# A due-time scheduler in a two-layer attention kernel: pacing of projection steps in cross attention

## The chip, the cores and the metric

The kernel runs on one core of one Trainium2 chip. The metric is the device time of one execution in microseconds (us); the times given are medians over the runs shown. The core's engines work in parallel, each in its own program order: PE (TensorE, matrix products; PEld are its weight loads), DVE (VectorE), ACT (ScalarE), POOL (GpSimd) and SP (SyncE, which here only issues DMA transfers). They wait for each other through semaphores.

## What is computed

Two layers of a transformer block, in float32, for 4 batches of 512 tokens of width 320, with 20 heads of width 16. Each layer is self attention, cross attention to a context of 1601 tokens of width 192, and a gated feed-forward stage:

```python
h1 = _ln(x, n1_g, n1_b)
x = _attn(h1, h1, q1, k1, v1, o1_w, o1_b, heads) + x
h2 = _ln(x, n2_g, n2_b)
x = _attn(h2, context, q2, k2, v2, o2_w, o2_b, heads) + x
h3 = _ln(x, n3_g, n3_b)
proj = h3 @ ff_w1 + ff_b1
a, g = jnp.split(proj, 2, axis=-1)
ff = a * jax.nn.gelu(g, approximate=False) @ ff_w2 + ff_b2
return ff + x
```

`_attn` projects queries, keys and values, takes `softmax(q k^T * dh**-0.5)` over the keys, multiplies with the values and projects with `wo`; `_ln` is a layer norm with scale and bias.

## The kernel before, in words

**Units.** The work is cut into 84 units, listed in order: for each layer 20 units of self attention and 20 of cross attention (4 batches by 5 groups of 4 heads; 64 columns of the projections to a group), then 4 feed-forward units. A cross unit has 13 chunks of up to 128 keys, a self unit 4. The Python program writes out every engine's instruction order by hand; there is no automatic scheduling behind it.

**A chunk** (`main`, the loop at its end) goes like this. First one round of products on PE: the scores of this unit's four heads, keys by queries (L1280; three passes a head, the last of which subtracts the row maxima kept in `nrows`), and woven between them the products of a later unit's heads, queries by keys (L1054, the last 65 keys L1081), whose row maxima are wanted before that unit may begin. PE works on four heads at a time, as each takes 32 rows. ACT raises the scores of the chunk (L1290, four instructions of 128x512). DVE reduces the products of the later unit to maxima (L1069, four instructions; L1091). Then come the values product of the chunk before (L1306), which ACT copies out (L1325; L1320 in chunk 0) and POOL adds to the unit's sum `o` (L1326, in chunks 1 to 12). Then `steps` runs some of the pending work.

**The maxima of the next unit.** `give` hands a chunk one pair of products for each half of its round, if the later unit's keys and queries have been moved four rounds ago (`at_hand`). A chunk without a pair leaves products over, and these are made up by an extra round (`round_of(extra[0])`) in another chunk. At the end of chunk 10, behind its steps, `max_reduce` and `max_end` finish the next unit's maxima on DVE: a reduction (L1109), a cast (L1119), a subtraction (L1120), both of 128x16 with their operands in SBUF, and a transpose (L1123); SP then copies them to `nrows` in four DMAs (L1131).

**Pending work** stands in eight queues (`chains`). Each entry has a cost (a rough PE time in us), a due round, a hard condition (`ready`) and a soft one (`soon`). There are two rounds to a chunk. `pick` takes, of the queues' first entries that may run, the one due first. The entries that cost 0.1 or more are the projection steps; in cross attention these are

- keys of a later unit, four pieces of 200 or 201 context columns (L951, copied out at L994 by DVE or L997 by ACT, whichever the program expects to be free sooner; after the fourth piece POOL splits them into a high and a low part, L803 and L804, 128x801, and four DMAs, L852, move them into place),
- its queries (L927, ACT L935, a split of 128x256 on POOL at L803 and L804, eight DMAs),
- values (L1015, copied out at L994 or L997), in two parts: the first for groups 0 and 1 (128 columns) and the second for groups 2 to 4 (192 columns), 13 steps each and batch,
- the output projection of an attention that has ended (L1209, added to `x` by DVE at L1216), eight steps a batch.

Entries of no cost or of 0.01 (`LIGHT`) are norms (statistics L546, normalisation L562 and L568), the context's transposes (L733), the affine part on POOL (L595), and the division. **The division**: when group 4 of a batch has ended, an errand loads the sums of the exponentials (L1158), DVE inverts them (`invert`), they are saved, another errand reads them back with the unnormalised output (L1183, L1184), and POOL multiplies (L1191, three instructions: the first two together, the third later). An errand is run by `carry`, at the end of `steps`, when the moves of keys and queries have left room in that round.

**Credit.** Each round adds to `clock["credit"]` what the due times ask for (`pace`, at least -2 and at most 4 in all), and each entry that runs takes its cost off. In `steps`, a step is run only if the credit is at least its cost times a factor: 0.5 for the first of a chunk, 0.75 for the second, 1.5 for the third, then 3.0 us. If the first of the queues cannot be afforded, `steps` ends for this chunk.

`add_proj` puts keys and queries into their queues three units ahead in cross attention (`u.early` marks the first cross unit of a layer, which is prepared during self attention); `add_values` puts in the two parts of the values.

Of the kernel before, what the change touches and what calls it, by code (L numbers as in the profile page):

```python
# [61 lines left out]
def slices(n, k):  # L62

    out, at = [], 0
    for i in range(k):
        w = n // k + (i < n % k)
        out.append((at, w))
        at += w
    return out


KCUT = slices(HALF, 4)
# [3 lines left out]
def kernel(ctx: ExitStack, tc: tile.TileContext, x, context, ws, out):  # L76
# [273 lines left out]
    units = []  # L350
# [29 lines left out]


    chains = {n: deque() for n in ("divide", "project", "norm", "scale", "context", "early", "proj", "values")}
    clock = {"round": 0, "credit": 0.0, "lights": 0, "tiles": None, "ff": False}
    ALIKE = ("project", "early", "proj", "values")
    LIGHT = 0.01
    stage = [0] * B
# [41 lines left out]
    def add(chain, cost, f, due, ready=yes, soon=yes):  # L428
        chains[chain].append((cost if isinstance(cost, tuple) else (cost,), due, ready, soon, f))
# [7 lines left out]
    def pick():  # L437
        heads = [
            (q[0][1] + late_by(n), n)
            for n, q in chains.items()  # L440
            if q and q[0][2]() and q[0][3]() and (q[0][0][0] != LIGHT or clock["lights"])
        ]
        return min(heads)[1] if heads else None

    def run(chain):
        costs, _, ready, _, f = chains[chain].popleft()
        assert ready(), chain
        f()
        clock["credit"] -= sum(costs)
# [19 lines left out]
    def tick():  # L469
        clock["round"] += 1  # L470
        clock["credit"] = max(-2.0, min(4.0, clock["credit"] + pace()))

    def steps(beside, lights=1):


        tick()
        clock["lights"] = lights
        clock["tiles"] = True if beside is None else None
        done = 0
        while True:  # L480
            name = pick()
            if name is None:
                break
            cost = sum(chains[name][0][0])
            if cost >= 0.1:
                share = (2.2, 1.1) if beside else (9.0, 9.0) if beside is False else (0.5, 0.75, 1.5)
                least = cost * share[done] if done < len(share) else 3.0
                if clock["credit"] < (3.0 if beside is False else least):
                    break
                done += 1  # L490
                if clock["tiles"] is not None:
                    clock["tiles"] = name in ALIKE
            run(name)
            if cost == LIGHT:
                clock["lights"] -= 1
        clock["tiles"] = None
        carry()
# [308 lines left out]
    def add_proj(u):  # L806
# [3 lines left out]
        keys_due = due - 10 if u.cross else due  # L810
# [55 lines left out]
        def keys_free():  # L866
            return not pending["k"]
# [110 lines left out]
        if not u.cross:  # L978
            for part in range(2):
                add(chain, (0.46,) * 3, lambda part=part: both(part), due - 2 + 2 * part, lambda part=part: part or staging_free())  # L980
        else:
            for part, (_, w) in enumerate(KCUT):
                add(
                    chain, 0.05 + w * 8 / 2400, lambda part=part: keys_of_context(part),
                    keys_due - 2 * (len(KCUT) - 1 - part), lambda part=part: part or keys_free(),
                )
            if u.g == 0:
                add(chain, 0.0, hold, due - 4, yes, lambda: "h" in u.own)
            add(chain, (0.477,) * 3, queries, due - 2, staging_free)
# [10 lines left out]
    def add_values(u):  # L1000

        parts_k = CK if u.cross else HK
        wv = wv2 if u.cross else wv1

        def values(i, c):

            h0, h1 = PARTS[i]
            w = (h1 - h0) * DH
            ps = bank("vps")
            r = min(P, u.nkeys - c * P)  # L1010
            written(0.1 + w * 4 * len(parts_k) / 2400, ps)
            at = c * P
            for k, _, n in parts_k:
                for f, m in tiles_of(r):
                    nc.tensor.matmul(  # L1015
                        ps[f : f + m, :w],
                        lhsT=u.kvT[:n, k, at + f : at + f + m],
                        rhs=wv[:n, k, h0 * DH : h1 * DH],
                        start=(k == 0),
                        stop=(k == len(parts_k) - 1),  # L1020
                    )
            taken(vals[:r, c, h0:h1, 0:DH], ps[:r, :w].rearrange("p (h d) -> p h d", d=DH), ps, 0.12 + w * 0.001)
            u.vmade[i] += 1

        for i, g in enumerate((0, 2)):

            user = attn[u.n - (4, 1)[i]] if u.n else None
            w = (PARTS[i][1] - PARTS[i][0]) * DH

            def free(c, user=user):  # L1030
                return u.kvT is not None and (user is None or user.valued > min(c, user.nch - 1))

            for c in range(u.nch):
                add(
                    "values", 0.05 + w / 600 * len(parts_k), lambda i=i, c=c: values(i, c),
                    units[u.i + g].start + 2 * c, lambda c=c, free=free: free(c),
                )


# [332 lines left out]
    def add_norms(i):  # L1372

        while norms and norms[0].i <= i + ((1 if norms[0].b else 3) if norms[0].kind == "ff" else AHEAD + 1 if norms[0].early else 8):
            u = norms.popleft()
            if u.kind == "ff":
                add_norm(u.l, u.b, 2, lambda t, u=u: setattr(u, "hT", t), lambda u=u: u in ff_read, u.start - (4 if u.b else 40))
            else:

                def done(u=u):  # L1380
                    return u.made["q"] == G and (u.cross or u.made["k"] == G and u.vmade[1] == u.nch)

                due = lead(u) - (10 if u.cross else 28)
                add_norm(u.l, u.b, int(u.cross), lambda t, u=u: u.own.update(h=t), done, due)
# [299 lines left out]
    for i, u in enumerate(units):  # L1684
        nxt = units[i + 1] if i + 1 < len(units) else None
        before(u)
        if u.kind == "ff":

            flush()
            now(loads)  # L1690
            loads.clear()
            until_normed(lambda: u.hT is not None)
        clock["ff"] = u.kind == "ff"
        add_norms(i)
        for k in (3, SOON, AHEAD):
            v = units[i + k] if i + k < len(units) else None
            if v is not None and v.kind != "ff" and k == (SOON if not v.cross else AHEAD if v.early else 3):
                add_proj(v)
                if v.g == 0:
                    add_values(v)  # L1700
        (ff_main if u.kind == "ff" else main)(u, giver(u), nxt)
# [27 lines left out]
```

## Time and profile before

| | before |
|---|---|
| time, median of 3 runs | 3000.69 us (3000.01 to 3001.19) |
| time of the profiled execution | 3000.91 us |
| its span, first to last instruction | 2999.1 us |
| mean granted clock of TensorE | 0.993 |
| cross attention of the first layer, about | 370 to 1232 us |
| cross attention of the second layer, about | 1850 to 2720 us |

The profile was taken of one execution. Its page gives busy time by engine, the clock that TensorE was granted, the chain of waits that ended last, and groups of equal instructions. In a row of the timeline stand start, duration, engine, line, operation, output and inputs with their shapes, and the count; in brackets the idle time of the engine before it and what ended it. In a row of busy time by stretch stand the stretch and its length, the busy time of PE, PEld, DVE, ACT and POOL with the instructions in brackets, the granted clock of TensorE as a share of full speed, the share of the DMA engines and their GB/s. In a row of a group stand the busy time, the mean duration in ns, and the idle time before.

### The profile page before, as it was taken

The page shows a single profiled execution, that of the slowest core. Times are in us where ns is not written, and L with a number is a line of the kernel's source. Part 1 is how long each engine was busy: PE and PEld are TensorE (multiplying, and loading weights), DVE is VectorE, ACT ScalarE, POOL GpSimd, SP SyncE. Part 2 cuts the span into 40 slices and gives each one's busy share as a digit, 9 for nine tenths or more (in the row PEclk, how much of TensorE's full clock was granted, in tenths as well). Part 3 has the DMA queues.
Part 4 walks back from the last instruction along what each step waited for, and adds up shares of the span by engine and source line. Part 5 has one row for each costly group of instructions (what it writes and reads, how often), then busy time and mean ns, then how long its engine had stood idle before and what let it go on. Part 6 is the DMA issues. An engine that isn't in the chain of part 4 may idle for free.

```text
span 2999.1 us, 84363 instructions
## 1 busy us (share of the span) xinstructions
PE 2885.4 (96%) x35018; PEld 1509.7 (50%) x35018; DVE 2150.8 (72%) x4143; ACT 1892.7 (63%) x3746; POOL 1194.0 (40%) x1305
## 2 busy tenths in 40 slices
PE   8999999999999999999999899999999999999999
PEld 4455554555554554355554555555555555544555
DVE  6877888889889888323268788888888888873221
ACT  3766677877877878501147676778778778784000
POOL 3444344544544545211224443445445454451110
PEclk9999999999999999999999999999999999999999
DMA  4444223132232122200123342222221121222000
GB/s 107 103 122 102 71 74 96 46 90 60 53 82 67 39 56 60 82 17 15 37 60 74 91 99 66 66 58 53 53 64 46 49 70 44 54 54 76 22 22 14
DMA packets 186543, 188.70 MB, mean 63 GB/s; under 512 B 69668, under 2 KB 137264, under 8 KB 186160
## 3 DMA queue, kind: packets, MB, share of 16 engines
q1 hardware_dynamic: 185368, 182.11, 24.0%
q8 instruction: 276, 4.52, 0.6%
q10 hardware_dynamic: 760, 1.18, 0.2%
q14 instruction: 107, 0.88, 0.1%
q0 software_dynamic: 32, 0.00, 0.0%
HBM read 55.76 MB, written 29.36 MB: 28 GB/s over the span
## 4 chain that ended last, share of the span: by engine, by line
PE 77%; DVE 18%; DMA 1%; issue 1%; ACT 1%; POOL 1%; SPq 1%; ACTq 0%; DVEq 0%; POOLq 0%
PE av L1306 21%; PE st L1280 15%; PE fps L1391 9%; DVE pm L1069 9%; PE sps L1054 6%; PE yps L1498 6%; PE vps L1015 4%; DVE nmax L1069 4%; PE ops L1209 3%; PE kps L951 3%; PE qkps L886 3%; PE fps L1451 2%; PE qps L927 2%; PE sps L1081 1%; DVE hturned L608 1%
## 5 line engine op out<-in xcount | busy, mean ns | idle before, releaser
L1290 ACT ACTIVATE pr<-st 128x512 f32<-128x512 f32 (+1 forms) x2720 | 1405.0, 603 | 429.1 <-PE st L1280 381.4
L1069 DVE TENSOR_REDUCE pm<-sps 128x1 f32<-128x512 f32 x1920 | 1185.3, 681 | 129.6 <-PE sps L1054 121.5
L1326 POOL TENSOR_TENSOR o<-o,vo 128x512 f32<-128x512 f32 x576 | 740.7, 1286 | 1125.9 <-ACT vo L1325 1114.3
L1054 PE MATMUL sps<-kT,q 32*128 32x512 f32 x4800 | 874.4, 429 | 13.7 <-DMA q<-low 4.3
L1306 PE MATMUL av<-pr,vals 128*32 128x512 f32 (+1 forms) x5440 | 738.4, 609 | 74.7 <-DVE nmax L1069 19.3
L1280 PE MATMUL st<-q,kT 32*128 32x512 f32 (+1 forms) x5120 | 795.7, 421 | 7.1 <-DVE pm L1069 6.4
L1280 PEld LDWEIGHTS st<-q,kT 32*128 32x128 f32 (+1 forms) x5120 | 422.9, 180 | 299.5 <-issue 120.1
L1280 PE MATMUL st<-nrows,ones 32*128 32x512 f32 (+1 forms) x2720 | 542.6, 399 | 5.4 <-DMA nrows<-turned 5.4
L1054 PEld LDWEIGHTS sps<-kT,q 32*128 32x128 f32 x4800 | 424.0, 183 | 102.2 <-DVE pm L1069 26.8
L1069 DVE TENSOR_REDUCE nmax<-sps 128x1 f32<-128x512 f32 x640 | 395.2, 680 | 81.1 <-PE sps L1054 77.9
L1325 ACT COPY vo<-av 128x512 f32<-128x512 f32 x576 | 352.3, 612 | 26.8 <-PE av L1306 24.7
L1462 ACT ACTIVATE gl<-fps,b 128x512 f32<-128x512 f32 x80 | 54.8, 687 | 414.3 <-PE fps L1451 303.0
L1306 PEld LDWEIGHTS av<-pr,vals 128*32 128x32 f32 (+1 forms) x5440 | 111.1, 108 | 348.8 <-DVE pm L1069 180.7
L1391 PE MATMUL fps<-hT,w 128*128 128x512 f32 x640 | 283.2, 597 | 0.0
L1280 PEld LDWEIGHTS st<-nrows,ones 32*128 32x128 f32 (+1 forms) x2720 | 247.0, 180 | 28.2 <-DMA nrows<-turned 4.8
L1463 DVE SCALAR_TENSOR_TENSOR hid<-fps,b,gl 128x512 f32<-128x512 f32 x80 | 59.7, 748 | 238.8 <-ACT gl L1462 236.7
L1391 PEld LDWEIGHTS fps<-hT,w 128*128 128x128 f32 x640 | 119.2, 190 | 155.1 <-issue 152.6
L1498 PE MATMUL yps<-w,hid 128*128 128x320 f32 x640 | 176.0, 435 | 0.1
L1498 PEld LDWEIGHTS yps<-w,hid 128*128 128x128 f32 x640 | 120.4, 190 | 56.4 <-ACT gl L1462 5.3
L1209 PEld LDWEIGHTS ops<-wo,aT 112*32 112x32 f32 (+1 forms) x3072 | 98.0, 110 | 64.6 <-issue 42.9
L1209 PE MATMUL ops<-wo,aT 112*32 112x160 f32 (+1 forms) x3072 | 126.2, 301 | 0.9 <-DVE pm L1069 0.9
L1505 DVE TENSOR_TENSOR x<-yps,x 128x320 f32<-128x320 f32 x32 | 15.7, 492 | 145.9 <-PE yps L1498 145.9
(89 smaller groups left out, 2476.1 us busy)
## 6 DMA issues: line engine op xcount, KB each, us to landing
kT<-stages SPq DMA_DIRECT2D x160, 200.2 KB
oway<-o SPq DMA_DIRECT2D x80, 256.0 KB
q<-high SPq DMA_DIRECT2D x160, 64.0 KB
q<-low SPq DMA_DIRECT2D x160, 64.0 KB
kT<-high SPq DMA_DIRECT2D x60, 128.0 KB
q<-high SPq DMA_DIRECT2D x60, 128.0 KB
kT<-low SPq DMA_DIRECT2D x57, 128.0 KB
aT<-oway SPq DMA_DIRECT2D x32, 224.0 KB
```

Of the source, the lines that this page charges most:

```text
L886: nc.tensor.matmul(ps[f : f + m, :w], lhsT=wqk[:n, k, f // GD, column : column + m], rhs=first.hT[:n, k, at : at + w], start=(k == 0), sto ...
L1015: nc.tensor.matmul(ps[f : f + m, :w], lhsT=u.kvT[:n, k, at + f : at + f + m], rhs=wv[:n, k, h0 * DH : h1 * DH], start=(k == 0), stop=(k == ...
L1054: nc.tensor.matmul(ps, lhsT=u.q[j * SLOT : (j + 1) * SLOT, e, t * P : (t + 1) * P], rhs=u.kT[j * SLOT : (j + 1) * SLOT, u.k0 + s * 512 : u ...
L1069: nc.vector.tensor_reduce(to[:, j : j + 1], ps, AX.X, ALU.max, negate=(ns == 1))
L1209: nc.tensor.matmul(ps[f : f + m, : D // 2], lhsT=aT[:n, k, f * NQ + t * SLOT : f * NQ + t * SLOT + m], rhs=wo[:n, k, cols], start=(k == 0) ...
L1280: nc.tensor.matmul(own[0][:r, :], lhsT=ones[rows, :r] if e == 2 else u.keys(rows, c), rhs=u.rows[rows, :] if e == 2 else u.q[rows, e, :], ...
L1290: nc.scalar.activation(p[:r], own[0][:r], AF.Exp)
L1306: nc.tensor.matmul(ps[j * SLOT : (j + 1) * SLOT, :], lhsT=columns_of[:r, head : head + SLOT], rhs=pr.pop((c, j))[:r, :], start=True, stop= ...
L1325: nc.scalar.copy(vo, ps)
L1326: nc.gpsimd.tensor_tensor(u.o, u.o, vo, ALU.add)
L1391: nc.tensor.matmul(ps, lhsT=w1[:, k, i * FF + c * P : i * FF + (c + 1) * P], rhs=natural(u.hT[:, k]), start=start, stop=stop,)
L1498: nc.tensor.matmul(ps[:, :D], lhsT=hid[c][:, t * P : (t + 1) * P], rhs=w2[:, c, :], start=(c == 0), stop=(c == NHC - 1),)
```

## The change

Three edits, none of which changes an instruction; they change which entries run in which chunk.

- **Share of credit in cross attention.** A flag `clock["cross"]` is set for each unit. In a cross unit's chunks the factors are -1.0, 1.0 and 1.5 instead of 0.5, 0.75 and 1.5: the first step runs unless the credit lies below minus its cost, the second needs its full cost.
- **Due rounds of the pieces of keys.** The four pieces of a cross unit's keys were due two rounds apart, counted back from the last; they are due five apart, but for the first cross unit of a layer. The last piece's due round stays.
- **Due rounds of the first part of the values.** In cross attention of batches 1 to 3 the steps of the first part are due 20 rounds sooner.

```diff
-    clock = {"round": 0, "credit": 0.0, "lights": 0, "tiles": None, "ff": False}
+    clock = {"round": 0, "credit": 0.0, "lights": 0, "tiles": None, "ff": False, "cross": False}
...
             if cost >= 0.1:
-                share = (2.2, 1.1) if beside else (9.0, 9.0) if beside is False else (0.5, 0.75, 1.5)
+                share = (2.2, 1.1) if beside else (9.0, 9.0) if beside is False else (-1.0, 1.0, 1.5) if clock["cross"] else (0.5, 0.75, 1.5)
                 least = cost * share[done] if done < len(share) else 3.0
                 if clock["credit"] < (3.0 if beside is False else least):
                     break
...
                 add(
                     chain, 0.05 + w * 8 / 2400, lambda part=part: keys_of_context(part),
-                    keys_due - 2 * (len(KCUT) - 1 - part), lambda part=part: part or keys_free(),
+                    keys_due - (2 if u.early else 5) * (len(KCUT) - 1 - part), lambda part=part: part or keys_free(),
                 )
...
                 add(
                     "values", 0.05 + w / 600 * len(parts_k), lambda i=i, c=c: values(i, c),
-                    units[u.i + g].start + 2 * c, lambda c=c, free=free: free(c),
+                    units[u.i + g].start + 2 * c - (20 if u.cross and g == 0 and u.b else 0), lambda c=c, free=free: free(c),
                 )
...
         clock["ff"] = u.kind == "ff"
+        clock["cross"] = u.cross
         add_norms(i)
```

## The prediction

> **What bounds the kernel now.** I read the page first, then busy time by stretch, then the timelines of single chunks. A unit is one group of four heads of one batch; I call a cross unit layer.batch.group, counted from 0, and its key chunks 0 to 12.
>
> ```profile
> span 2999.1 us, 84363 instructions
> PE 2885.4 (96%) x35018; PEld 1509.7 (50%) x35018; DVE 2150.8 (72%) x4143; ACT 1892.7 (63%) x3746; POOL 1194.0 (40%) x1305
> ...
> PE 77%; DVE 18%; DMA 1%; issue 1%; ACT 1%; POOL 1%; SPq 1%; ACTq 0%; DVEq 0%; POOLq 0%
> ```
>
> PE sets the end, and where it does not, DVE does. The change acts in cross attention, about 1700 of the 2999 us. Two 800 us stretches of it, then units 0.1.1, 0.1.2 and 0.1.3:
>
> ```profile
> core 0: us, PE busy (x) PEld busy (x) DVE busy (x) ACT busy (x) POOL busy (x), PEclk, DMA share, GB/s
> 400.00:1200.00 800.00, 770.80 (x10925) 406.03 (x10923) 693.40 (x1307) 627.05 (x1253) 390.43 (x382) 1.00 0.26 66
> 1900.00:2700.00 800.00, 772.45 (x10935) 405.39 (x10928) 677.43 (x1259) 632.73 (x1266) 392.71 (x382) 1.00 0.22 55
> ...
> 647.30:693.50 46.20, 44.73 (x696) 24.43 (x695) 40.38 (x84) 34.41 (x69) 20.81 (x19) 1.00 0.30 77
> 693.50:740.60 47.10, 44.04 (x660) 23.41 (x659) 43.31 (x85) 34.91 (x70) 20.91 (x29) 1.00 0.33 81
> 740.60:779.80 39.20, 38.64 (x536) 20.15 (x535) 31.55 (x60) 33.70 (x67) 24.62 (x24) 1.00 0.19 46
> ```
>
> PE stands idle for 29.2 and 27.6 us of the two stretches, 57 us in all: with PE's work unchanged, that and time at a lower clock are all there is to win. The first question is therefore whether moving steps out of crowded chunks into empty ones pays by itself. Two empty chunks (no step) of unit 0.3.3, and what a key step costs:
>
> ```profile
> 1181.18 2.07 ACT L1290 ACTIVATE pr<-st 128x512 f32<-128x512 f32 x4 [0.24 <-PE st L1280]
> 1183.10 0.62 ACT L1325 COPY vo<-av 128x512 f32<-128x512 f32 x1
> 1183.70 2.07 ACT L1290 ACTIVATE pr<-st 128x512 f32<-128x512 f32 x4
> ...
> 1186.43 1.08 ACT L1290 ACTIVATE pr<-st 128x512 f32<-128x512 f32 x2 [0.19 <-PE st L1280]
> ```
>
> ```profile
> 562.30 0.86 PE L951 MATMUL kps<-ctxT,w 96*32 96x200 f32 x16
> ```
>
> A chunk lasts from one group of exponentials to the next: 2.52 us, then 2.73. ACT's own work is 2.07 + 0.62 = 2.69, so an empty chunk is held by ACT and not by PE, but by only 2.63 (the mean) against 2.52. A step adds about its PE time in an empty chunk and in a crowded one alike. Spreading alone is worth about 0.1 us a chunk, so the answer must lie in single stalls.
>
> **The dearest repeated stall** is in chunks 10 and 11 of group 0 of batches 1 to 3 in both layers, six units. In unit 0.1.0 (POOL, DVE, PE, ACT in turn):
>
> ```profile
> 638.75 1.28 POOL L1326 TENSOR_TENSOR o<-o,vo 128x512 f32<-128x512 f32 x1 [1.73 <-ACT vo L1325]
> 639.99 2.52 POOL L1191 TENSOR_TENSOR aT<-aT,rT 112x512 f32<-112x512 f32 x2
> ...
> 639.09 0.98 DVE L1119 CAST parts<-nmax 128x16 fp32r<-128x16 f32 x1
> 640.11 1.21 DVE L1120 TENSOR_TENSOR parts<-nmax,parts 128x16 f32<-128x16 f32 x1
> ...
> 642.18 0.44 PE L1280 MATMUL st<-q,kT 32*65 32x512 f32 x2 [1.10 <-DVE pm L1069]
> ...
> 639.37 2.06 ACT L1290 ACTIVATE pr<-st 128x512 f32<-128x512 f32 x4 [0.69 <-PE st L1280]
> 643.58 2.05 ACT L1290 ACTIVATE pr<-st 65x512 f32<-65x512 f32 x4 [1.67 <-PE sps L1054]
> ...
> 647.31 1.08 ACT L1290 ACTIVATE pr<-st 128x512 f32<-128x512 f32 x2 [0.90 <-PE st L1280]
> ```
>
> max_end's cast ends at 640.07, as POOL's add ends at 640.03; its subtraction, 16 columns, then takes 1.21 us and ends at 641.32 with the first of the two divisions (639.99 + 1.26). DVE stands behind POOL, no bank is emptied, and PE waits 1.10. Chunk 11 lasts 643.58 - 639.37 = 4.21 us. An empty chunk 11 without a division, in unit 0.1.3:
>
> ```profile
> 768.57 2.07 ACT L1290 ACTIVATE pr<-st 128x512 f32<-128x512 f32 x4 [0.85 <-PE sps L1081]
> ...
> 771.17 2.07 ACT L1290 ACTIVATE pr<-st 128x512 f32<-128x512 f32 x4
> ...
> 773.75 2.07 ACT L1290 ACTIVATE pr<-st 128x512 f32<-128x512 f32 x4
> ```
>
> It lasts 2.58, so the hold costs 1.63. In unit 0.2.0 a second price follows:
>
> ```profile
> 855.90:859.30 3.40, 2.26 (x22) 0.77 (x15) 3.37 (x6) 1.73 (x4) 3.40 (x3) 1.00 0.22 58
> 859.30:862.70 3.40, 3.40 (x26) 1.08 (x25) 2.74 (x5) 2.25 (x5) 0.17 (x1) 0.63 0.31 89
> 862.70:866.10 3.40, 3.31 (x46) 1.41 (x40) 2.04 (x4) 1.84 (x5) 1.27 (x1) 0.87 0.09 31
> ...
> 859.31 2.05 ACT L1290 ACTIVATE pr<-st 65x512 f32<-65x512 f32 x4 [1.68 <-PE sps L1054]
> ...
> 864.64 1.57 ACT L1290 ACTIVATE pr<-st 128x512 f32<-128x512 f32 x3 [1.56 <-PE st L1280]
> ```
>
> After 3.4 us with 1.14 us of idle PE the clock falls to 0.63 and 0.87; chunk 12 lasts 5.33 against 647.31 - 643.58 = 3.73 in unit 0.1.0, 1.60 more.
>
> **The change part by part.** The order of both programs tells what moves. PE, POOL and SP issue the same instructions as before; a net five of the 432 copies of keys and values out of banks go from ACT to DVE, too few to price.
>
> The share of credit: of 520 cross chunks, 138 were empty and 60 took two steps; now 128 and 48. It is little, because the first step still waits while credit is below minus its cost. Ten fewer empties at 0.11 (0.2 where the next chunk pays too): **-1.5 us**.
>
> The key pieces, due five rounds apart: keys land earlier, so that chunks seldom lack their pair of maximum products, which an extra round makes up. Cross chunks with an extra round fall from 18 to 8; four of the ten only completed a chunk with half its pair and are costed at nothing (PE's products are the same, 0.2 either way). A whole one:
>
> ```profile
> 810.17 2.06 ACT L1290 ACTIVATE pr<-st 128x512 f32<-128x512 f32 x4 [0.23 <-PE sps L1081]
> ...
> 814.39 2.06 ACT L1290 ACTIVATE pr<-st 128x512 f32<-128x512 f32 x4 [0.48 <-PE st L1280]
> ...
> 817.73 2.05 ACT L1290 ACTIVATE pr<-st 65x512 f32<-65x512 f32 x4 [0.48 <-PE st L1280]
> ...
> 605.36 2.06 ACT L1290 ACTIVATE pr<-st 128x512 f32<-128x512 f32 x4 [0.66 <-PE st L1280]
> ...
> 608.33 2.07 ACT L1290 ACTIVATE pr<-st 128x512 f32<-128x512 f32 x4 [0.42 <-PE st L1280]
> ```
>
> The chunk with a value step and an extra round lasts 4.22, its partner with a key step and no pair 771.17 - 768.57 = 2.60, together 6.82; a plain key chunk (814.39 to 817.73) and a plain value chunk (605.36 to 608.33) 3.34 + 2.97 = 6.31. So 0.51, four times net, the other two of the six being replaced by whole rounds in group 1 of batch 0: **-2.0 us**.
>
> The earlier values, together with the other two, move the division. On SP the load of the sums (L1158) now stands behind the eight query moves that it preceded, so that invert, read and divide follow later. POOL's order in unit 0.2.0 around its adds (L1326; the x6 ends with add 9, and so does, after, the single one):
>
> ```
> before: L1326 x6 | L1191 x2 | L1326 x3 | L1191 | L803 L804 801 wide
> after:  L803 L804 801 wide | L1326 | L803 L804 256 wide | L1326 x3 | L1191 x2
> ```
>
> The pair goes from between add 9 and add 10, where max_end runs, to chunk 0 of the next unit, where DVE has reductions only, in all six units. Five holds go at 1.63 (8.15), with the 1.60 of clock; in unit 1.1.0 chunk 11 had a key step, and I count only what PE waited for the maxima:
>
> ```profile
> 2137.32 0.50 PE L1280 MATMUL st<-nrows,ones 32*128 32x512 f32 x2 [1.41 <-DMA nrows<-turned]
> ```
>
> In the new SP order those four copies go ahead of the division's loads. What POOL has near max_end instead are the splits:
>
> ```profile
> L803 POOL CAST stages<-stages 128x801 fp32r<-128x801 f32 x40 | 34.2, 856 | 43.3 <-ACT stages L997 16.6 <-DVE stages L994 10.9 <-DVE pm L1069 8.7
> L804 POOL TENSOR_TENSOR stages<-stages 128x801 f32<-128x801 f32 x40 | 64.1, 1603 | 3.2
> L803 POOL CAST high<-low 128x256 fp32r<-128x256 f32 x18 | 7.5, 419 | 0.3 <-ACT low L935 0.3
> ```
>
> In five units the key split stands before add 9, a chunk too early, and a query split behind it, in a chunk that the query step lengthens: 0 to 0.42 each; I take 0. In unit 0.1.0 it stands right behind add 9, so the subtraction waits for its 0.86. Together 8.15 + 1.60 + 1.41 - 0.86 = **-10.3 us**; if the splits hold fully (5 x 0.42), -8.2.
>
> The Trainium skill ("TensorE: Matmul & The Clock Gate", section The HAM clock gate) lets the clock drop after an idle window of about 3.4 us. Here 1.14 us of idle in such a stretch was followed by 0.63, so the trace differs; by the page the sum would lack the 1.60, and come to -8.7.
>
> Unpriced are the normalisation chunks of group 2: unit 0.1.2 is at 43.31 of 47.10 on DVE and now takes 18 steps instead of 15, unit 0.1.1 11 instead of 16. The six steps that move either fill PE's 3.1 idle us of unit 0.1.2 or stand behind DVE; I take 0, with 3 us either way over all such units, and one clock drop more or less.
>
> Sum: -1.5 - 2.0 - 10.3 = -13.8. The profiled execution took 3000.91 us (span 2999.1), 0.2 above the median of 3000.69; 3000.91 - 13.8 = 2987.1, as a median **2987 us**.
>
> **Rivals.**
> A, DVE decides in group 2. Eight such units (two layers, four batches) take normalisation with values and output projections in the same chunks. If each gains one stall of 1.1 us of idle PE and the 1.60 of clock, that is 8 x 2.7 = 21.6, and 2987 + 21.6 = 3009, slower. It decides from five such stalls on. For it: DVE's 92% there. Against: unit 0.1.1 is relieved, and the empty chunk behind the normalisation is now filled.
> B, POOL's holds only change their owner: the 801-wide split of 1.60 takes the place of the division's 1.26 at max_end. For it: it moves to chunks 8 to 10. Against: it is a chunk ahead. Then the 10.3 is nought: 2997. The Trainium skill ("SBUF — State Buffer", section Who interferes with whom) speaks for it: a DVE instruction with two SBUF inputs is blocked for the whole of any GpSimd instruction that reads SBUF, the splits among them; the 1.21 us agrees.
> C, the change hardly does what it says: 128 empties instead of 138, and the saved rounds come back as other waits: 3000.
> D, stalls go beyond the six, as filled chunks hide half of the 57 - 10 us of other idle that lies in empty ones (a quarter of all chunks): 47 x 0.25 x 0.5 = 6, and two further clock drops of 1.6: 2987 - 9 = 2978.
>
> **How the numbers follow.** A change under 0.2% (6 us) can't be told from none. Forecast 0.50, A 0.13 (a third of it within 0.2%, as a part of the stalls may come), B 0.15, C 0.07, D 0.15. Faster by over 0.2% holds the forecast, D, and little of B: 0.67; within 0.2%: 0.22; slower: 0.11. The forecast's own range is 2981 to 2993 (the splits' 2.1, the 3 us, a clock drop). The range to 8 in 10 takes in D and B: 2974 to 3002.
>
> **What would show it.** In the profile after: L1120 at the end of chunk 10 of those six units at about 0.2 us instead of 1.2, but near 0.9 in unit 0.1.0; no PE wait of 1.1 us there; chunk 11 near 2.6; the divisions beside reductions in chunk 0; PE idle of the cross stretches below 57 us by 8 to 12. It is wrong if L1119 and L1120 stay long beside L804, if group 2 units grow beyond 50 us, or if PEclk drops below 1 in more stretches than before.

## The result and the profile after

| | before | after |
|---|---|---|
| median | 3000.75 us (2997.77 to 3003.13, 6 runs) | 3021.14 us (3016.97 to 3029.77, 6 runs) |
| profiled execution | 3000.91 us, span 2999.1 | 3029.77 us, span 3028.0 |
| first exponentials of unit 0.0.0 to those of 0.3.4 | 828.9 us | 843.7 us |
| the same from 1.0.0 to 1.3.4 | 824.4 us | 833.1 us |

The change makes the kernel slower: 1.0073 times as long, 95% interval 1.0058 to 1.0088. The profiled execution is the slowest of the six, 28.9 us longer than that of before: the two stretches of cross attention (read from ACT's L1290) hold 23.5 us of this, and some 5 us were lost ahead of cross attention.

The page of the profile after: the span, busy time by engine, and the shares of the chain of waits.

```profile
span 3028.0 us, 84314 instructions
PE 2888.1 (95%) x35018; PEld 1511.9 (50%) x35018; DVE 2159.4 (71%) x4148; ACT 1892.8 (63%) x3741; POOL 1191.8 (39%) x1305
...
PE 74%; DVE 19%; DMA 3%; issue 1%; ACT 1%; POOL 1%; SPq 1%; DVEq 0%; ACTq 0%; POOLq 0%
```

PE has the same work (2888.1 against 2885.4 us). What grew is DMA on the chain, from 1% to 3%. Busy time by stretch after, the same two stretches as in the prediction:

```profile
400.00:1200.00 800.00, 755.24 (x10740) 398.35 (x10740) 680.51 (x1281) 612.12 (x1224) 379.23 (x373) 0.99 0.26 66
1900.00:2700.00 800.00, 760.41 (x10892) 400.82 (x10887) 684.96 (x1265) 618.76 (x1232) 384.54 (x376) 1.00 0.22 56
```

The same columns for two shorter stretches of the second:

```profile
core 0: us, PE busy (x) PEld busy (x) DVE busy (x) ACT busy (x) POOL busy (x), PEclk, DMA share, GB/s
2379.50:2386.30 6.80, 5.80 (x73) 2.63 (x67) 4.41 (x8) 5.84 (x12) 4.76 (x4) 1.00 0.83 238
2386.30:2389.70 3.40, 2.23 (x13) 0.69 (x17) 2.66 (x5) 1.09 (x2) 0.00 (x0) 0.73 0.63 186
```

PE's idle time in the two 800 us stretches rose from 57 to 84 us (44.8 + 39.6). The shorter stretches are one of the places, in unit 1.2.1. Its timeline after shows the end of POOL's split of the keys (L804), SP issuing the four moves of these keys out of the staging buffer (L852), then DVE's copy of the next unit's first key piece into that buffer:

```profile
2370.91 1.60 POOL L804 TENSOR_TENSOR stages<-stages 128x801 f32<-128x801 f32 x1
...
2374.10 2.65 SPq L1131 DMA_DIRECT2D nrows<-turned  x4
...
2376.79 0.62 SPq L1183 DMA_DIRECT2D aT<-oway  x1
...
2379.50 3.35 SPq L852 DMA_DIRECT2D kT<-stages  x4
...
2383.30 0.87 PE L951 MATMUL kps<-w 96*32 96x201 f32 x16
...
2387.04 0.37 DVE L994 COPY stages<-kps 128x201 f32<-128x201 f32 x1 [2.96 <-DMA kT<-stages]
2387.33 2.47 DVE L1069 TENSOR_REDUCE pm<-sps 128x1 f32<-128x512 f32 x4
...
2387.47 0.50 PE L1054 MATMUL sps<-kT,q 32*128 32x512 f32 x1 [2.17 <-DVE stages L994]
```

The piece is computed by 2384.17 (2383.30 + 0.87). The DMA engines, 0.92 busy at 259 GB/s in the 3.4 us from 2379.5, still read the buffer; the wait ends at 2387.04, 7.54 us after the first move was issued. DVE stands for 2.96 us with the maxima (L1069) behind it, so banks stay full and PE stands for 2.17; the granted clock then falls to 0.73. This chunk took 7.32 us. The waits after 380 us, grouped (waiting instruction, releaser, total us, count, longest):

```profile
DVE stages L994 <- DMA kT<-stages: 17.4, 8, 3.1
...
PE sps L1054 <- DVE stages L994: 11.4, 8, 2.3
...
DVE stages L733 <- DMA ctxT<-stages: 6.7, 2, 3.4
...
DVE stages L733 <- DMA stages<-in_ctx_dram: 4.4, 2, 2.7
...
ACT stages L997 <- DMA kT<-stages: 2.1, 1, 2.1
```

None of the first, third, fourth and fifth stands in the trace before. In the order of the program these nine first pieces stand four rounds behind the last move of keys, where before they stood eight behind it. Four rounds alone do not make the wait: before, six other pieces stood as close, as in unit 1.2.4:

```profile
2491.34 3.46 SPq L852 DMA_DIRECT2D kT<-stages  x4
...
2502.62 0.37 DVE L994 COPY stages<-kps 128x201 f32<-128x201 f32 x1 [0.33 <-issue]
```

There the moves go out as soon as the keys are split, and the copy comes 10.3 to 11.3 us after the first of them. In the nine places after, SP comes to the moves only 2.7 to 7.5 us after the split has ended; in unit 1.2.1 the split ends at 2372.51, and ahead of the moves stand the copies to `nrows`, which start at 2374.10, and four loads of the division (L1183, L1184). The nine waits end 6.2 to 8.4 us after the first move. Five pieces of cross attention that stand only two rounds behind a move, which there goes out at once, have no such wait. So the wait has two parts, a piece that was drawn closer and a move that SP issues late. `keys_free` asks whether the program has put the moves into SP's queue, not whether they have landed.

The context's transposes (L733) form a second group, in layer 0 only. In unit 0.1.1 after:

```profile
664.21 0.60 SPq L741 DMA_DIRECT2D ctxT<-stages  x1
...
668.58 0.64 DVE L733 STREAM_TRANSPOSE stages<-stages 128x192 f32<-128x192 f32 x2 [3.42 <-DMA ctxT<-stages]
...
669.85 1.06 PE L1306 MATMUL av<-pr,vals 128*32 128x512 f32 x8 [3.34 <-DVE pm L1069]
```

The save of a turned context (L741) stood behind queries' moves in SP's queue, each 0.6 us, until 664.21; DVE waits 3.42 us for it to leave its buffer, and PE 3.34.

The holds that the prediction expected to go are still there. Unit 0.2.0 after, end of chunk 10 (POOL, DVE, ACT):

```profile
867.37 1.60 POOL L804 TENSOR_TENSOR stages<-stages 128x801 f32<-128x801 f32 x1
...
868.48 0.52 DVE L1119 CAST parts<-nmax 128x16 fp32r<-128x16 f32 x1
...
868.93 1.29 POOL L1326 TENSOR_TENSOR o<-o,vo 128x512 f32<-128x512 f32 x1
...
869.03 1.21 DVE L1120 TENSOR_TENSOR parts<-nmax,parts 128x16 f32<-128x16 f32 x1
...
869.87 2.06 ACT L1290 ACTIVATE pr<-st 128x512 f32<-128x512 f32 x4 [0.48 <-PE st L1280]
...
873.05 2.05 ACT L1290 ACTIVATE pr<-st 65x512 f32<-65x512 f32 x4 [0.16 <-PE st L1280]
```

The division is gone from here. The split of the keys (L804) takes POOL until 868.97 and pushes its add (L1326) into max_end, whose subtraction waits for the add: 1.21 us again. Group by group the 23.5 us are, summed over the units of both layers: group 0 of batches 1 to 3 -6.9, group 1 +8.6, group 2 +7.4, group 3 +14.5, group 4 -1.6, the first unit of each layer +1.5 together.

### The profile page after: what moved, and what is told of

Same layout as the page of the kernel before. It is cut to its first block, busy times and chain, and to the rows that moved or that the text cites. A ratio compares the mean times of both kernels' runs of the same rounds, so it can differ in the third digit from the quotient of the medians.

```text
span 3028.0 us, 84314 instructions
## 1 busy us (share of the span) xinstructions
PE 2888.1 (95%) x35018; PEld 1511.9 (50%) x35018; DVE 2159.4 (71%) x4148; ACT 1892.8 (63%) x3741; POOL 1191.8 (39%) x1305
## 4 chain that ended last, share of the span: by engine, by line
PE 74%; DVE 19%; DMA 3%; issue 1%; ACT 1%; POOL 1%; SPq 1%; DVEq 0%; ACTq 0%; POOLq 0%
PE av L1306 20%; PE st L1280 14%; PE fps L1391 9%; DVE pm L1069 9%; PE yps L1498 6%; PE sps L1054 6%; PE vps L1015 4%; DVE nmax L1069 3%; PE ops L1209 3%; PE kps L951 3%; PE qkps L886 3%; PE fps L1451 2%; PE sps L1081 1%; PE qps L927 1%; DMA kT<-stages 1%
## 5 line engine op out<-in xcount | busy, mean ns | idle before, releaser
L1290 ACT ACTIVATE pr<-st 128x512 f32<-128x512 f32 (+1 forms) x2720 | 1405.3, 604 | 447.9 <-PE st L1280 398.5
L1069 DVE TENSOR_REDUCE pm<-sps 128x1 f32<-128x512 f32 x1920 | 1187.0, 681 | 119.8 <-PE sps L1054 111.3
L1326 POOL TENSOR_TENSOR o<-o,vo 128x512 f32<-128x512 f32 x576 | 739.9, 1284 | 1158.9 <-ACT vo L1325 1133.8
L1054 PE MATMUL sps<-kT,q 32*128 32x512 f32 x4800 | 871.1, 431 | 22.9 <-DVE stages L994 11.4
L1306 PE MATMUL av<-pr,vals 128*32 128x512 f32 (+1 forms) x5440 | 739.7, 610 | 88.2 <-DVE pm L1069 24.5
L1069 DVE TENSOR_REDUCE nmax<-sps 128x1 f32<-128x512 f32 x640 | 395.8, 681 | 83.8 <-PE sps L1054 70.3
L886 PE MATMUL qkps<-hT,wqk 96*32 96x256 f32 (+1 forms) x1920 | 120.2, 392 | 0.0
```

The lines of the kernel that those rows point to most:

```text
L886: nc.tensor.matmul(ps[f : f + m, :w], lhsT=wqk[:n, k, f // GD, column : column + m], rhs=first.hT[:n, k, at : at + w], start=(k == 0), sto ...
L1054: nc.tensor.matmul(ps, lhsT=u.q[j * SLOT : (j + 1) * SLOT, e, t * P : (t + 1) * P], rhs=u.kT[j * SLOT : (j + 1) * SLOT, u.k0 + s * 512 : u ...
L1069: nc.vector.tensor_reduce(to[:, j : j + 1], ps, AX.X, ALU.max, negate=(ns == 1))
L1290: nc.scalar.activation(p[:r], own[0][:r], AF.Exp)
L1306: nc.tensor.matmul(ps[j * SLOT : (j + 1) * SLOT, :], lhsT=columns_of[:r, head : head + SLOT], rhs=pr.pop((c, j))[:r, :], start=True, stop= ...
L1326: nc.gpsimd.tensor_tensor(u.o, u.o, vo, ALU.add)
```

## The experiments

Theory W: what the change loses it loses mainly at the copy that waits for the moves of keys. The rivals are the holds at max_end, SP's queue with the context's transposes, and the order of the steps itself. The results of all twelve, with before and after; the last two columns are the two cross stretches of the first table, read from the one profiled execution of each kernel, while the medians are over all runs. Each ratio is to runs of before made beside that kernel, whose medians were 3000.0 to 3001.4 us.

| kernel | median us | ratio to before, 95% interval | layer 0 | layer 1 |
|---|---|---|---|---|
| before | 3000.75 | | 828.9 | 824.4 |
| share alone | 3007.59 | 1.0021 (1.0011 to 1.0031) | 833.4 | 828.6 |
| values alone | 2995.74 | 0.9981 (0.9972 to 0.9990) | 822.6 | 823.2 |
| keys alone | 3004.48 | 1.0013 (1.0004 to 1.0023) | 828.6 | 826.3 |
| share + keys | 3003.11 | 1.0007 (0.9998 to 1.0017) | 828.9 | 822.8 |
| share + values | 3020.26 | 1.0067 (1.0049 to 1.0085) | 846.1 | 821.8 |
| keys + values | 2988.07 | 0.9958 (0.9943 to 0.9973) | 818.5 | 819.6 |
| all three (after) | 3021.14 | 1.0073 (1.0058 to 1.0088) | 843.7 | 833.1 |
| after, guard of six rounds | 2993.63 | 0.9979 (0.9969 to 0.9988) | 822.1 | 820.7 |
| after, two buffers | 3003.28 | 1.0013 (1.0003 to 1.0022) | 834.4 | 822.0 |
| after, two buffers, later transposes | 2998.81 | 0.9995 (0.9985 to 1.0004) | 830.5 | 822.5 |
| before, max_end as reductions | 2979.74 | 0.9928 (0.9911 to 0.9944) | 818.9 | 813.8 |
| keys + values, max_end as reductions | 2977.26 | 0.9924 (0.9910 to 0.9939) | 815.2 | 813.6 |
| guard of six rounds, max_end as reductions | 2972.35 | 0.9904 (0.9887 to 0.9920) | 811.3 | 811.0 |

### A guard at the first key piece

```diff
+                moved_at[of] = clock["round"]
...
                     keys_due - (2 if u.early else 5) * (len(KCUT) - 1 - part), lambda part=part: part or keys_free(),
+                    lambda part=part: part or clock["round"] >= moved_at["k"] + 6,
```

> The changed kernel with one condition more: the first of a unit's four key pieces waits until six rounds (three chunks) have gone by since the last move of keys was issued. Theory W (the copy of the next keys into the staging buffer waits, on DVE or ACT, for the DMA that still reads the keys before out of it): those waits, 19.5 us in the profile after, fall below 2 us and the time to 2997 to 3005. Rival H (the key split on POOL now holds max_end's subtraction in more units): splits and max_end stand as they did, so 3015 or more. Rival S (the share of credit crowds group 2 units): the steps per chunk hardly change, so 3015 or more.

2993.63 us, 3 us below W's range: 27 us come back, and no copy waits on kT<-stages. That speaks for W; the rivals had 3015 us or more. But the guard also changes which step runs in which chunk, so it can't say by itself that it was the wait.

### One edit left out at a time

Without the values' edit (share + keys):

> The change without its third edit (the values' first part is due as before). Theory W: within the cross units no first key piece now follows a move of keys within two rounds, so few waits of the copies for the DMA, and 2996 to 3004, the divisions' holds of the kernel before being back. Rival S: the share is as in the change, 3012 or more. Rival H: splits are as near to max_end as in the change, 3012 or more.

Without the keys' edit (share + values):

> The change without its second edit (pieces of keys due two rounds apart, as before). Theory W: four first pieces in cross units still follow a move within two rounds, half as many as in the change, so about half the loss, 3005 to 3013. Rival S: as the change, 3015 or more. Rival H: splits come later again, 3000 or less.

Without the share's edit (keys + values):

> The change without its first edit (the old shares of credit). Theory W: one first piece in a cross unit follows a move within two rounds, so 2997 to 3005. Rival S: the loss is gone, 2990 to 3000. Rival H: as the change, 3012 or more.

Share + keys (3003.11) lies in W's range. Share + values (3020.26) lies above it and in that of rival S; keys + values (2988.07) lies 9 us below W's and 2 below S's. Neither carries all three: S had 3012 or more for share + keys. W counted the first pieces two rounds behind a move; share + values has four of them, as expected, and none waits.

Share + keys is as before, keys + values is faster than before, share + values loses 19.5 us without one wait on kT<-stages. So the share and the values together bring a second loss that is not W, all of it in layer 0 (846.1 against 828.9). A part of it is to be seen in SP's queue. In unit 0.0.1, share + values (SP, then PE):

```profile
469.22 2.58 SPq L218 DMA_DIRECT2D lng<-in_L_xattn_n_g_dram  x3
471.85 1.88 SPq L218 DMA_DIRECT2D lnb<-in_L_xattn_n_b_dram  x3
473.83 2.67 SPq L1131 DMA_DIRECT2D nrows<-turned  x4
...
477.70 0.49 PE L1280 MATMUL st<-nrows,ones 32*128 32x512 f32 x2 [3.38 <-DMA nrows<-turned]
```

The same place before:

```profile
468.89 2.69 SPq L1131 DMA_DIRECT2D nrows<-turned  x4
471.62 1.93 SPq L218 DMA_DIRECT2D lng<-in_L_xattn_n_g_dram  x3
473.60 1.88 SPq L218 DMA_DIRECT2D lnb<-in_L_xattn_n_b_dram  x3
```

With the share changed, six small loads of a layer norm's scale and bias are issued ahead of the four copies that the next unit cannot start without, and PE stands 3.38 us. The transposes account for another 8.3 us of DVE there (5.0 on saves, 3.3 on loads). After itself does not have the stand at 477; it has the transposes. A part of the second loss goes with the clock. Two stretches of share + values at a granted clock of 0.50:

```profile
478.40:485.20 6.80, 6.75 (x55) 2.70 (x52) 4.11 (x8) 3.98 (x9) 1.27 (x1) 0.50 0.23 52
509.10:519.30 10.20, 9.83 (x65) 3.95 (x69) 6.82 (x12) 3.33 (x7) 1.27 (x1) 0.50 0.19 42
```

With three of 3.4 us each (from 676, 888 and 1014 us) they make 27 us of layer 0, against 7 us before (from 505 and 860 us). If PE does half its work in the 20 us more, some 10 of the 17.2 us that layer 0 lost go that way (an estimate).

### The wait alone taken away

```diff
             low, high = room["low"], room["high"]
+            if u.m % 2:
+                low = w1_flat[:, 2 * D + 2 * TOK : 2 * D + 2 * TOK + HALF]
```

Units alternate between two staging buffers; every engine's order of instructions is that of after.

> The kernel after, in the same order of instructions, but units alternate between two staging buffers for keys, so that the first piece's copy (L994, L997) has no transfer to wait for. Theory W (the copy's wait on the moves of the keys before it is the main loss): no wait of L994 or L997 on kT<-stages is left (17.4 and 2.1 us after), the layer 1 cross units come back from 833 to 820-826, layer 0 stays at 833 or more, since the waits of the context's transposes (6.7 and 4.4 us) are untouched, and the time is 3000 to 3010. Rival Q (the delay is in SP's queue and only shows at the copy): the wait appears elsewhere and the time stays at 3014 or more. Rival O (the guard of the first experiment gained by another order of steps, not by the wait it removed): no waits on kT<-stages, but 3014 or more.

3003.28 us, 17.9 less than after, within theory W's range, and both rivals fall. In the nine places SP issues the moves as late as after, 2.7 to 7.4 us behind the split, but the copies now come 4.5 to 6.7 us after the first move and wait for none. The chunk of unit 1.2.1 that took 7.32 us after (busy time of that chunk after, then of the same chunk with two buffers):

```profile
2385.20:2392.50 7.30, 5.13 (x52) 2.16 (x49) 3.42 (x7) 2.73 (x6) 2.33 (x2) 0.77 0.47 126
```

```profile
2368.10:2371.30 3.20, 3.11 (x48) 1.56 (x44) 2.85 (x6) 2.54 (x5) 1.66 (x2) 1.00 0.47 115
```

The same chunk takes 3.20 us at full clock, with the DMA engines as busy (0.47). By groups the gain sits where the waits were: 13.0 us in group 1 and 7.3 in group 3; group 2 is the same to 0.1. The eight waits of PE behind L994 were 11.4 us; the rest, with ACT's copy and the lower clock that followed three of the waits, was not taken apart. The transposes' waits are left, 5.2 us on saves and 4.3 us on loads.

Layer 1 is then 2.4 us faster than before, layer 0 5.5 slower.

### Each edit alone

> The kernel before with the values' due date alone changed. Theory V (the gain of 12 us that values and keys show together comes from the values, which take the division pair off POOL under max_end): 2986 to 2992. Rival B (both are needed: pieces of keys must go too before a division moves): 2996 to 3002. Theory W expects no copy that waits on kT<-stages, but one or two short ones, since only one first piece stands two rounds behind a move.

> The kernel before with the keys' spacing alone changed. The prediction had -2 us for it: 2996 to 3000. Rival K (the keys carry the gain that keys and values show together): 2986 to 2992. Rival L (sooner keys alone bring the copies behind the moves): 3004 or more, with waits on kT<-stages of over 5 us in sum.

> The kernel before with the shares alone changed. Theory N (the share costs nothing by itself and loses only together with the sooner values, as its 20 us beside them and 3 us beside the keys suggest): 2998 to 3004, no waits on kT<-stages, waits of L733 on transfers under 3 us. Rival S (the share itself costs): 3010 or more, with waits of the context's transposes of 6 us and more in layer 0. Rival G (the prediction: fewer idle rounds): 2994 to 2998.

All three missed. Values alone gain 5.6 us, between the two theories and at the edge of B's; keys alone lose 3 to 4, the time of rival L without its waits (1.1 us on kT<-stages); the share alone loses 6.2, between its two theories. With keys alone the six group 0 units lose 8.8 us: the cast there takes 1.28 us or more and the subtraction 1.20, chunk 11 lasts 4.49 to 4.50 us, and in five of the six a granted clock of 0.67 or 0.68 follows, with a chunk 12 of 5.17 to 5.33 us; in the sixth the clock stays at 1.00 after the same chunk 11, and chunk 12 takes 3.69. The six group 0 units show also what the values do (unit 0.2.0 of the kernel with values alone; POOL, DVE):

```profile
856.41 0.17 DVE L1119 CAST parts<-nmax 128x16 fp32r<-128x16 f32 x1
...
856.58 1.29 POOL L1326 TENSOR_TENSOR o<-o,vo 128x512 f32<-128x512 f32 x1 [2.14 <-ACT vo L1325]
...
856.62 1.27 DVE L1120 TENSOR_TENSOR parts<-nmax,parts 128x16 f32<-128x16 f32 x1
...
857.81 2.52 POOL L1191 TENSOR_TENSOR aT<-aT,rT 112x512 f32<-112x512 f32 x2
```

The division stands behind max_end now, yet the subtraction is held as long, by the add. These units gain 8.6 us, in chunk 10 (2.55 us in place of 3.24 in five of them) and chunk 12 (2.68 to 3.63 in place of 3.71 to 5.34), which have lost their key steps; one of these now stands in chunk 11, which the hold lengthens anyway (4.02 us with the step, 4.22 without). The share alone has 7.3 us of PE waits for `nrows`, the longest 4.1 at 478 us, and in unit 1.0.2 a stretch from 2001 to 2010 at clock 0.50, right after two normalisations in one chunk (54.7 us for the unit, 47.7 before). Beside the values its price is 24.5 us (2995.74 to 3020.26), beside keys and values 33.

### The hold taken away

```diff
-        nc.vector.tensor_copy(high.bitcast(F32R), of)
-        nc.vector.tensor_tensor(low, of, high, ALU.subtract)
+        nc.vector.tensor_reduce(high.bitcast(F32R), one, AX.X, ALU.max)
+        nc.vector.tensor_reduce(less.bitcast(F32R), one, AX.X, ALU.max, negate=True)
+        nc.vector.tensor_reduce(low, both.rearrange("p (z j t) -> p j t z", z=2, t=NQ), AX.X, ALU.add)
```

`one` is the maxima with an axis of length 1 behind; `less` is the second half of a buffer `both`, whose first half is the maxima.

> The kernel before; max_end's cast and subtraction are written as three reductions over one input each, which add one small instruction to DVE for each of its 59 calls. The prediction's theory of the hold (DVE's subtraction waits out POOL's instruction, and PE waits for DVE): none of the reductions runs over 0.4 us, the six gaps of PE of 1.1 us ahead of st (642, 858, 1077, 2348, 2414, 2563 us) are gone, and the time is 2986 to 2995, that is the prediction's 10 us less what 59 more instructions of some 0.2 us cost where DVE is the limit. Rival (the hold lies beside other waits of the same length): 2997 to 3003, with the gaps still there behind another releaser. Rival (what holds DVE is not tied to the form of the instruction): the reductions are held for 1.2 us too, and the time is 3000 to 3008.

2979.74 us, 20.6 below before: twice what the prediction gave the six holds, and below the expected range. The groups of max_end before, and then of this kernel (busy us, mean ns):

```profile
L1119 DVE CAST parts<-nmax 128x16 fp32r<-128x16 f32 x80 | 40.9, 511 | 1.5
...
L1120 DVE TENSOR_TENSOR parts<-nmax,parts 128x16 f32<-128x16 f32 x80 | 23.3, 291 | 2.7
```

```profile
L1124 DVE TENSOR_REDUCE parts<-nmax 128x16 f32<-128x32 f32 x80 | 15.0, 188 | 2.8
L1122 DVE TENSOR_REDUCE parts<-nmax 128x16 fp32r<-128x16 f32 x80 | 13.1, 164 | 1.5
L1123 DVE TENSOR_REDUCE nmax<-nmax 128x16 fp32r<-128x16 f32 x80 | 12.7, 159 | 0.0
```

Three instructions take 40.8 us where two took 64.2 (80 calls in the whole run; the expectation counted those behind 380 us), and beside 23.4 us less of DVE stand 20.6 us less of time. The cast, 511 ns in the mean for 16 columns, was held too: in cross attention it took over 0.25 us in 31 of 38 calls, elsewhere in 7 of 42. Unit 0.1.0 of this kernel (POOL's add, then DVE):

```profile
640.39 1.29 POOL L1330 TENSOR_TENSOR o<-o,vo 128x512 f32<-128x512 f32 x1 [1.75 <-ACT vo L1329]
...
640.73 0.17 DVE L1122 TENSOR_REDUCE parts<-nmax 128x16 fp32r<-128x16 f32 x1
...
640.82 0.16 DVE L1123 TENSOR_REDUCE nmax<-nmax 128x16 fp32r<-128x16 f32 x1
641.01 0.19 DVE L1124 TENSOR_REDUCE parts<-nmax 128x16 f32<-128x32 f32 x1
...
641.37 4.83 DVE L1069 TENSOR_REDUCE pm<-sps 128x1 f32<-128x512 f32 x8
...
641.63 2.54 POOL L1195 TENSOR_TENSOR aT<-aT,rT 112x512 f32<-112x512 f32 x2
```

All of it runs beside the add: the next maxima start 0.64 us after the first reduction (640.73 to 641.37), where before the cast and the subtraction alone took from 639.09 to 641.32. The Trainium skill ("SBUF — State Buffer", section Who interferes with whom) names copies and casts in a two-port mode, and instructions with two SBUF inputs beside a GpSimd instruction that reads SBUF, as those with which VectorE and GpSimd lock each other out, and says that `tensor_reduce` never does on this chip; the trace agrees, 0.16 to 0.19 us beside a running add. The six group 0 units gain 7.9 us (the prediction had 10.3 for them), the eight of group 2 another 6.0, the other cross units 6.6 together. The price of 1.63 us for a hold was right: chunk 11 takes 2.57 to 2.60 us in five of the six, 4.22 before. But chunk 12 then takes 4.38 to 4.42 in these five, 3.71 to 3.73 before in four of them, so that a part comes back.

> The kernel of keys and values (2988.07 us) with the same three reductions, tried as the fastest. By the theory of the hold its nine held subtractions and its held casts go as well: 2976 to 2985. If the holds lie beside other waits: 2986 to 2991. If the third instruction costs more than the holds: over 2991.

2977.26 us, 10.8 below keys + values: within the range of the theory of the hold, near its fast end. That it is 10.8 and not 20.6 would follow if keys and values had already won a part of the same time; this was not tested apart.

### The transposes

```diff
-            add("context", LIGHT, lambda i=i: turn(i), at, yes, lambda i=i: clock["round"] >= ctx_in[b, i][1] + 4)
+            add("context", LIGHT, lambda i=i: turn(i), at, yes, lambda i=i: clock["round"] >= ctx_in[b, i][1] + 8)
```

> The kernel after with two staging buffers, and a context's next transposes eight rounds behind the issue of their load instead of four (only layer 0 has them; a few steps of its chunks change places with it). Theory T (what layer 0 still loses is the wait of the transposes L733 for loads and saves that stand behind queries' moves in SP's queue, 9.5 us of DVE): waits of L733 on transfers under 2 us, layer 0's cross units down from 834 to 825-830, layer 1 as it was at 822, the time 2994 to 2999. Rival (layer 0's loss lies in the order of its steps): 3001 or more with the waits gone. Rival (the wait only moves to the next reader of the contexts): as much wait at L935 or L951 on ctxT, and 3001 or more.

The waits of L733 are gone, and the time is 4.5 us below that with two buffers; the two intervals still touch (1.0003 to 1.0004), so the gain is likely, not certain. Layer 0 came down by 3.9 us to 830.5, just short of the 825 to 830 expected, and another wait grew, from 1.3 to 6.1 us:

```profile
PE st L1282 <- DMA nrows<-turned: 6.1, 5, 1.8
```

Theory T holds in part; a part of SP's delay seems only to have changed its customer.

### The whole change, with both obstacles away

> The whole change with both of its obstacles out of the way: the first key piece stands six rounds behind the last move of keys (2993.63 us so far) and max_end is three reductions. If the holds cost it what they cost before (20 us, 3000.32 to 2979.74): 2970 to 2977, the fastest. If it is as with keys and values (2988.07 to 2977.26, 11 us), where part of the holds lay beside other waits: 2980 to 2985. In either case no copy waits on kT<-stages.

2972.35 us, the lowest median of all, 0.9904 times before (0.9887 to 0.9920; the interval overlaps that of keys + values with reductions), with no copy waiting on kT<-stages. Removing the holds is worth 21.3 us here (2993.63 to 2972.35). Against before with the same max_end (2979.74) the guarded change still gains 7.4.

## Why the prediction was wrong, step by step

It forecast 2987 us, in 2974 to 3002; the result is 3021. The sum was -13.8 and the result +20.4.

- **"-1.5 us" for the share** is the step that failed most, and in sign. The share costs 6.2 us alone, 24.5 beside the values and 33 beside keys and values. The step counted chunks that change their number of steps (138 empties to 128) and not what else moves with them. Of the 33 us, 17.9 come back with two buffers in the same order: they are the copies that wait for the staging buffer, which keys + values alone do not have. The prediction noted one change of SP's order, and took it as harmless; the moves of keys, the saves of contexts and the copies to `nrows` that stand late on SP had no price in it. What of this the transposes cost after is some 4 us; the rest is only partly placed.
- **The sum** added three terms as if each stood alone. The two other terms came to -12.3, and keys + values measured -12 (3000.02 to 2988.07). That is luck: the terms are wrong one by one, as follows.
- **"-2.0 us" for the key pieces** counted the earlier keys as a gain alone. It never asked what the earlier first piece overwrites: the staging buffer, which the moves of the keys before still read, nor when SP comes to these moves. With the share, nine first pieces stand four rounds behind moves that are issued late, and wait 19.5 us. Even alone the keys' edit cost 3 to 4 us, at longer holds and a lower clock.
- **"-10.3 us" for the division pair.** The mechanism was right: the hold costs time on the path, as the reductions show (7.9 us in those six units). That it would go was wrong, in keys + values too, where all six subtractions still take 1.26 us or more. The step said that the key split stands "a chunk too early" and took 0. It asked whether the split itself meets max_end; the split holds the cast and pushes the add, and the add meets the subtraction. L1120 took 1.21 us or more in five of the six units (0.76 in 0.1.0, where 0.9 was forecast), and six more such holds appeared, in group 3 of batches 0 to 2: the two instructions take 69.5 us after (40.4 + 29.1) where they took 64.2 before. Chunk 11 came to 3.16 to 3.35 us in five units and not 2.6. The six units still became 6.9 us shorter, as chunk 12 (2.56 to 2.86 us) has lost its key step.
- **The cast** had no term: it was read as the instruction ahead of the hold, though its own row showed 0.98 us for 16 columns.
- **The clock.** The price of 1.60 for a stall's lower clock was right in kind, and worked the other way: after the three longest new stands of PE behind these copies (1.49, 2.17 and 2.33 us, at 2267, 2387 and 1108 us) the clock fell to 0.50. It stayed at 1.00 after the six others (0.82 to 1.35 us at PE). Cross attention had 24 us at a clock of 0.50, 10 before.
- **The rivals.** B told the change of owner rightly, but at no loss against before (2997). A foresaw a loss in group 2 from DVE at its limit; group 2 did grow past 50 us in two units (1.1.2 and 1.2.2, 50.3 each), by 7.4 us over its eight units, a third of A's 21.6, and the two buffers leave it as it is. The loss that decided, a buffer still being read, stood in no rival.
- **What would show it.** PE's idle time was to fall by 8 to 12 us; it rose by 28. All three signs of being wrong came: L1119 and L1120 stayed long beside L804 (0.52 and 1.21 us above), group 2 units passed 50 us, and the clock fell below 1 in five stretches of cross attention against three.

What stays open: the 19.5 us of share + values, which lie in layer 0. Two of its places are shown (the copies to `nrows`, the transposes), and the time at half clock; how much each is worth, and what the rest is, was not taken apart. After with two buffers has only 5.5 us of loss in layer 0, so after is not the sum of this loss and of W. Nor is it shown why the nine waits for the buffer come only with all three edits.

## What to carry to other kernels

When steps are pulled forward, ask of each buffer that they write who reads it last, and whether the guard waits for that read's issue or its end: a guard on the issue is enough only while the schedule is loose and the issuer is not late (by up to 7.5 us here). Look for small instructions with long times (16 columns in 0.5 us): they are waits in disguise, and one written in another form was worth more here than all moving of steps. Price an edit to a schedule by all that it shifts in the in-order queues, the issuer of transfers among them, and not by the steps that it names. Edits to one schedule do not add up: two that gained 12 us together lost 20 with the third.

## What the runs showed of the hardware

- A cast with one SBUF input is held beside POOL's instructions like the two-input subtraction: 511 ns in the mean, up to 1.30 us, against 164 for the same cast written as a reduction.
- Four moves of 200 KB each, out of SBUF and into it, kept a copy waiting for their source until 6.2 to 8.4 us after the first issue (nine cases in the kernel after).
- A stand of PE of 2.17 us was followed by a granted clock of 0.73 in the mean of 3.4 us (at 2386 us in the kernel after), 1.14 us of idle time before by 0.63. A stall does not always bring it: with keys alone, chunks with 1.7 us of idle PE were followed by 0.67 or 0.68 in five units and by 1.00 in the sixth.
